# The opening of an edge-gated graph kernel, written in another order

## The chip, the core and the metric

The kernel runs on one core of one Trainium2 chip. Its time is the device time of one execution in microseconds (us); several executions are timed, and the median is given. A profile is one further execution, recorded by the hardware profiler. TensorE is PE in the profile (PEld is its weight load), VectorE is DVE, ScalarE is ACT, GpSimd is POOL, and SyncE, which only issues transfers here, is SP.

## The reference

There are 16 graphs (batch b) over the same 1024 nodes, with 256 features per node, and one adjacency matrix `adj` of 1024 x 1024 of which only some entries are not zero: about one in 128, and the diagonal.

```python
pre_u = einsum('bud,dk->buk', h, W1[:d]);  pre_v = einsum('bvd,dk->bvk', h, W1[d:])
hidden = relu(pre_u[:, :, None] + pre_v[:, None] + b1)
S = sigmoid(einsum('buvk,ko->buvo', hidden, W2)[..., 0] + b2)
a = einsum('buv,bud->bvd', S * adj, h)
m = einsum('uv,bud->bvd', adj, h) * h
z = beta1 * h + beta2 * (a @ Wa + ba) + beta3 * (m @ Wm + bm)
```

The gate S is only needed where `adj[u, v]` is not zero. So the kernel works on lists of edges.

## The kernel before, in words

The nodes v are cut into 8 tiles of 128 (`NT`), the 16 graphs into 4 groups of 4 (`GB`). A block is one group with one tile; there are 32. Each block takes ten steps (`T`), so the main loop (L745) has 320 steps. In a step, 128 edges, one in each partition, are worked on for four graphs at once: GpSimd gathers for each edge the row of its source node u from a table in DRAM (`fetch`, L494; a row holds `h W1[:d]` and `h` of the four graphs, 8 KB), TensorE spreads the rows of the target nodes v over the edges with a 0/1 matrix, the marks (`expand`, L564), DVE adds both and does relu and the product with W2 (`gate`, L598; L601 and L606), ACT does the sigmoid and scales the left factors (L609, L612), and TensorE sums the edges into their targets (`aggregate`, L614). Six fetches are under way at once (`NF`).

Before the first step, an opening of its own (L505 to L546) has to provide:

- **Edge lists** (`lists`, L239) of the first four tiles of v; the other four are made during the loop. A list is made in nine pieces, separated by `yield`: (1) the key is a row of 1024 adjacency entries per partition; DVE turns it into numbers (L249), ACT counts (L252); (2) DVE takes maxima in eight strips (L258); (3) DVE picks the top candidates and completes a tile `R` (L263 to L282); (4) TensorE sums over partitions (L286); (5) DVE computes the first slot and the number held (L291 to L309); (6) DVE writes the marks into a tile `made`, which has one buffer (L312, L319), ACT casts them to bytes (`few`, L329, two buffers), and DVE writes `RR` (L331); (7) four transfers write the bytes to `whose` (L335), TensorE multiplies the marks with `RR` (L338), ACT copies the product to `L` (L342); (8) DVE computes indices `uidx` and `vidx` (L346 to L364); (9) DVE writes one-hot rows (L370).
- **Row products** (`rows`, L434): for each of eight tiles of u, in two halves, TensorE multiplies `hT` with `w_u` (L427), and ACT copies the half out (L443). The finished tile is written to the table by SP (L446); the row of `h` itself gets there by a transfer from DRAM to DRAM (`copy_h`, L421).
- **Target rows of the first block** (`halves`, L452): two halves on TensorE with a bias product (L431, L427), each copied by ACT into `X` and `low` (L461, L462); then DVE subtracts (L463), and ACT writes the remaining three pieces of `X` (L465, L468).
- **Edge values** (`fetch_val`, L379): ten gathers by GpSimd of 128 adjacency values each.
- **Six fetches**, which wait until the whole table of the first group is in DRAM.

The order is written out by hand; nothing is rearranged later (`manual_schedule`, L471). Each engine works in order of issue, and a piece that waits holds what is behind it on its engine. The opening's order is the `script` (L518). A digit takes list 0 to 3 one piece further, `r` does one half of a row product, `h` one piece of `halves`, `v` the edge values (and the bias row `b1_p`, by `spread`, L190), and `f` issues the six fetches. What is registered with `after` for a step is done at that step's start; each string is one step. Row copies to the table are thus issued one step after a tile's second half. Of list 3 the last three pieces follow in loop steps 0, 2 and 4 (`advance`, L722).

The loads at the start are issued in the order of L508 to L513. The keys of lists 0 and 1 come by GpSimd's queue, those of lists 2 and 3 by SP's queue between the eight loads of `hT` (L241). After the script, `load_mark(0)` (L740) has ACT read the first marks back from `whose`, `expand` is called for steps 0 and 1, and the loop starts.

The PSUM banks `misc` (two) hold row products and halves, so the third product waits until ACT has copied the first. The banks `pc` (two) hold list products, and later the expansions.

Of the kernel before, what the change touches and what calls it, by code (L numbers as in the profile page):

```python
# [7 lines left out]
FP = mybir.dt.float32  # L8
FR = mybir.dt.float32r
# [4 lines left out]
P = 128  # L14
# [3 lines left out]
def kernel(  # L18
# [42 lines left out]
    nc = tc.nc  # L61
    B, N, D = x.shape
# [6 lines left out]
    NW = P // W  # L69
    TW = 5  # L70
    E = TW * P
# [113 lines left out]
    unit = fixed([P, P], "unit", FR)  # L185
# [9 lines left out]
    b1_p = fixed([P, D], "b1_p", FR)  # L195
# [6 lines left out]
    whose = const.tile([P, NT * NW, E], mybir.dt.uint8, name="whose")  # L202
# [9 lines left out]
    big = main.enter_context(tc.tile_pool(name="big", bufs=2))  # L212
# [4 lines left out]
    psa = main.enter_context(tc.tile_pool(name="psa", bufs=1, space=bass.MemoryType.PSUM))  # L217
# [12 lines left out]
    EARLY = 4  # L230
# [7 lines left out]

    def lists(vt):  # L239
        key = fetched[vt + 1][:, :N] if vt < EARLY else big.tile([P, N], FP, name="key", bufs=1)  # L240
        (nc.sync if 2 <= vt < EARLY else nc.gpsimd).dma_start(key, adjT[vt * P:(vt + 1) * P, :])  # L241
        yield "load"
        R = wk.tile([P, RC], FP, name="R", bufs=4)
        top = R[:, 5:5 + S]
# [2 lines left out]
        for c in range(0, N, N if vt < EARLY else N // 2):  # L247
            c = slice(c, c + (N if vt < EARLY else N // 2))
# [36 lines left out]
        for i in range(4):  # L285
            nc.tensor.matmul(pw[:, i:i + 1], sums[:, i].rearrange("p w q v -> p (w q v)"), R[:, 0:1],  # L286
                             start=True, stop=True)
# [23 lines left out]
        mark = big.tile([P, E], FP, name="made", bufs=1)  # L311
# [14 lines left out]
        RR = wk.tile([P, NW, RC], FP, name="RR", bufs=2)  # L326
        few = wk.tile([P, E], mybir.dt.uint8, name="few", bufs=2)
        yield "slot"
        nc.scalar.copy(few, mark)  # L329
        for w, mine in enumerate((soon, late)):  # L330
            nc.vector.tensor_scalar(RR[:, w, :], R, mine, None, ALU.mult)  # L331
        yield "step"
        for w in range(NW):
            for h in range(2):
                (nc.gpsimd if vt < EARLY else nc.scalar).dma_start(whose[h * W:(h + 1) * W, vt * NW + w, :], few[w * W:(w + 1) * W])  # L335
# [158 lines left out]
    def fetch(n):  # L494
        k, g, vt, w, j = where(n)
        nc.gpsimd.indirect_dma_start(  # L496
            out=fetched[n % NF], out_offset=None, in_=table[g],
            in_offset=bass.IndirectOffsetOnAxis(ap=uidx[:, vt * NW + w, j:j + 1], axis=0),
            bounds_check=N - 1, oob_is_err=False)
# [15 lines left out]
    for i in range(COPIES):  # L515
        copy_h(turn[i], nc.sync)

    script = ("r 0 0", "r r 0", "r 1", "0 r 1 1", "0 0 r r", "1 r 0 2 2", "r r 0 0 v 2", "1 1 r r",  # L518
              "2 r 1 r", "2 2 r r 1 1 h", "2 h 3 3", "2 2 h 3", "f h h 3", "3 3")
    m = 0  # L520
    piece = None
    parts = halves(0)
    for t, turns_ in enumerate(script):
        step = t - 100
        do(step)
        for c in turns_.split():
            if c == "r":
                if m % 2 == 0:
                    piece = rows(turn[m // 2], tabs[m // 2] if m // 2 < len(tabs) else None)
                    next(piece)  # L530
                go(piece, step)
                if m % 2 == 0 and m // 2 + COPIES < NT:
                    copy_h(turn[m // 2 + COPIES], nc.sync)
                m += 1
            elif c == "h":
                go(parts, step)
            elif c == "v":
                fetch_val(T)
                spread(b1_p, b1_b)
                next(parts)  # L540
            elif c == "f":
                for n in range(NF):
                    fetch(n)
            else:
                next(made[int(c)], None)
    do(len(script) - 100)  # L546
# [7 lines left out]

    marks, pcs, accs, evs, hbs, LTs, lefts = {}, {}, {}, {}, {}, {}, {}

    def load_mark(q):  # L560
        marks[q] = big.tile([P, E], FR, name="mark")
        nc.scalar.copy(marks[q], whose[:, order[q // NW][1] * NW + q % NW, :])  # L562

    def expand(n):  # L564
        k, g, vt, w, j = where(n)
# [171 lines left out]
    plan(again, ((103,), (113,), (125,), (133,)))  # L737
    begun = set(turn[:NT])
    end = parts = piece = last = None
    load_mark(0)  # L740
    for n in range(2):
        expand(n)
    left_adj(0)
# [200 lines left out]
```

## Time and profile before

| | |
|---|---|
| time, median of 3 runs | 1175.09 us (1167.8 to 1177.88) |
| span of the profiled execution, first to last instruction | 1165.8 us |
| PE, DVE, ACT, POOL busy | 1092.1, 1056.2, 893.5, 439.9 us |
| first `t` of the loop (L601) starts | 71.62 us |
| first, tenth after it, twentieth after it | 71.62, 112.31, 155.01 us |
| first fetch issued (L496) | 56.66 us |
| first product of TensorE (L427) | 5.94 us |

The page gives no time of its own for the profiled execution beside its span; the three timed runs lie 2.0 to 12.1 us above that span. A line of the timeline shows the start in us from the beginning of the span, the duration in us, engine, line, operation, output and input with sizes, how many instructions were merged, and in brackets how long the engine had been idle before, and what ended the wait. Where several conditions were waited for, the named one is the last by the profile. A windows line shows the stretch, its length, busy time of PE, PEld, DVE, ACT and POOL with the number of instructions, the granted TensorE clock as a share of full speed, the mean busy share of the 16 DMA engines, and GB/s.

### The profile page before, as it was taken

The numbers are of one execution on the slowest core, as the hardware profiler recorded it, in microseconds if no ns is written. First come the engines' busy times: TensorE is split into PE (matmuls) and PEld (weight loads), VectorE is DVE, ScalarE is ACT, GpSimd is POOL, SyncE is SP. The second block draws the span as 40 slices with busy tenths as digits, with TensorE's granted clock in tenths as the row PEclk, the third lists the DMA queues.
The fourth block names the chain that finished last, engine by engine and source line by source line (L and its number), as shares of the span: only waits on it lengthen the run. The fifth ranks groups of instructions, "written<-read, shape, count | busy, mean of one in ns | idle before, by whom it ended". The sixth has DMA issues, their size and how long they took to land. (4 is left out here: it accounts for less than half of the span.)

```text
span 1165.8 us, 23918 instructions
## 1 busy us (share of the span) xinstructions
PE 1092.1 (94%) x7633; PEld 723.1 (62%) x7633; DVE 1056.2 (91%) x3487; ACT 893.5 (77%) x2624; POOL 439.9 (38%) x428
## 2 busy tenths in 40 slices
PE   7867899999999999999999999999999999999986
PEld 6744666666666666666666666666666666666553
DVE  7688889888999989999999999999999999999994
ACT  2346587767887878888888888888888888888873
POOL 1556645253335333443333333333333333333330
PEclk9868899999999999999999999999999999999999
DMA  9986898999999999999999999999998998999991
GB/s 286 298 307 223 277 372 312 362 320 331 342 320 323 396 379 336 358 350 402 389 374 369 355 364 356 360 364 383 371 375 324 361 322 333 334 339 328 328 346 60
DMA packets 147048, 391.40 MB, mean 336 GB/s; under 512 B 16753, under 2 KB 105329, under 8 KB 110705
## 3 DMA queue, kind: packets, MB, share of 16 engines
q0 software_dynamic: 50016, 300.50, 68.9%
q1 hardware_dynamic: 81616, 74.99, 20.0%
q10 hardware_dynamic: 15280, 14.29, 3.7%
q8 instruction: 63, 1.03, 0.3%
q14 instruction: 73, 0.59, 0.1%
HBM read 393.78 MB, written 50.33 MB: 381 GB/s over the span
## 5 line engine op out<-in xcount | busy, mean ns | idle before, releaser
L496 POOL DMA_INDIRECT fetched<-table,uidx x320 | 341.5, 1067 | 628.3 <-PE acc L623 447.2
L606 DVE SCALAR_TENSOR_TENSOR t<-t,w_b 128x256 f32<-128x256 f32 x1280 | 478.3, 421 | 19.3 <-ACT left L612 0.5
L601 DVE TENSOR_TENSOR t<-fetched,pc 128x1024 f32<-128x1024 f32 x320 | 389.3, 1217 | 41.4 <-PE pc L569 13.9
L623 PE MATMUL acc<-fetched,left 128*32 128x256 f32 x4096 | 336.2, 391 | 31.9 <-ACT left L612 26.2
L612 ACT ACTIVATE left<-left,gt 128x32 f32<-128x32 f32 (+1 forms) x1280 | 299.3, 304 | 10.4
L569 PE MATMUL pc<-X,mark 128*128 128x512 f32 x640 | 237.6, 453 | 6.2 <-ACT mark L562 5.0
L623 PEld LDWEIGHTS acc<-fetched,left 128*32 128x32 f32 x4096 | 130.6, 109 | 179.3 <-issue 52.4
L569 PEld LDWEIGHTS pc<-X,mark 128*128 128x128 f32 x640 | 97.2, 191 | 140.0 <-issue 89.3
L609 ACT ACTIVATE gt<-sc,b_b 128x4 f32<-128x4 f32 x320 | 96.2, 301 | 43.4 <-DVE t L606 40.8
L672 PE MATMUL misc<-w_m,LT 128*128 128x256 f32 x496 | 117.2, 379 | 0.0
L672 PE MATMUL misc<-w_a,LT 128*128 128x256 f32 x496 | 117.1, 379 | 0.0
L579 ACT ACTIVATE left<-onehot,val 128x128 f32<-128x128 bf16 (+1 forms) x320 | 116.5, 364 | 0.0
L427 PE MATMUL misc<-w_v,hT 128*128 128x256 f32 x448 | 107.3, 383 | 0.0
L427 PE MATMUL misc<-w_u,hT 128*128 128x256 f32 x416 | 101.2, 390 | 5.7 <-ACT few L329 3.6
L606 DVE DVE_READ_ACCUMULATOR t<-t,w_b 128x1 f32 x1280 | 104.0, 81 | 0.0
L672 PEld LDWEIGHTS misc<-w_a,LT 128*128 128x128 f32 x496 | 93.9, 189 | 15.1
L672 PEld LDWEIGHTS misc<-w_m,LT 128*128 128x128 f32 x496 | 93.8, 189 | 14.9
L382 POOL DMA_INDIRECT val<-in_adjT_dram,vidx x80 | 85.7, 1071 | 35.1 <-issue 22.4
L427 PEld LDWEIGHTS misc<-w_v,hT 128*128 128x128 f32 x448 | 86.0, 192 | 13.9
L427 PEld LDWEIGHTS misc<-w_u,hT 128*128 128x128 f32 x416 | 79.5, 195 | 17.3 <-ACT few L329 3.7
L631 ACT COPY ev<-acc 128x512 f32<-128x512 f32 x128 | 75.5, 590 | 14.6 <-PE acc L623 4.2
L675 ACT COPY z<-misc 128x512 f32<-128x512 f32 x62 | 36.3, 586 | 58.1 <-PE misc L672 38.8
(164 smaller groups left out, 947.9 us busy)
## 6 DMA issues: line engine op xcount, KB each, us to landing
h_blk<-in_x_dram SPq DMA_DIRECT2D x31, 512.0 KB
out_dram<-z SPq DMA_DIRECT2D x31, 512.0 KB
hT<-in_xT_dram SPq DMA_DIRECT2D x28, 512.0 KB
table<-in_x_dram ACTq DMA_DIRECT2D x24, 512.0 KB
table<-tab SPq DMA_DIRECT2D x24, 512.0 KB
fetched<-table,uidx POOLq DMA_INDIRECT x320
table<-in_x_dram SPq DMA_DIRECT2D x8, 512.0 KB
table<-fetched SPq DMA_DIRECT2D x8, 512.0 KB
```

What stands on the lines that cost most here:

```text
L382: nc.gpsimd.indirect_dma_start(out=val[:, i, j:j + 1], out_offset=None, in_=adj_flat, in_offset=bass.IndirectOffsetOnAxis(ap=vidx[:, i, j: ...
L427: nc.tensor.matmul(p[:, bb * D:(bb + 1) * D], hT[:, 2 * h + bb, i, :], wt[:, i, :], start=(i == 0 and not begun), stop=(i == DC - 1), skip ...
L496: nc.gpsimd.indirect_dma_start(out=fetched[n % NF], out_offset=None, in_=table[g], in_offset=bass.IndirectOffsetOnAxis(ap=uidx[:, vt * NW ...
L569: nc.tensor.matmul(pcs[n][:, c], marks[n // TW][:, j * P:(j + 1) * P], cuts[k][:, w, c], start=True, stop=True)
L579: nc.scalar.activation(lefts[n][:, :m, :, 0, :], onehot[:, i, o:o + m, :].unsqueeze(2).to_broadcast([P, m, GB, V]), AF.Copy, scale=val[:, ...
L601: nc.vector.tensor_tensor(t, fetched[n % NF][:, :GD].rearrange("p (b d) -> p b d", b=GB), pcs.pop(n).rearrange("p (b d) -> p b d", b=GB), ...
L606: nc.vector.scalar_tensor_tensor(t[:, b, :], t[:, b, :], 0.0, w2_b, ALU.max, ALU.mult, accum_out=sc[:, b:b + 1])
L609: nc.scalar.activation(gt, sc, AF.Sigmoid, bias=b2_b)
L612: nc.scalar.activation(lefts[n][:, :m, b, 1, :], lefts[n][:, :m, b, 0, :], AF.Copy, scale=gt[:, b:b + 1])
L623: nc.tensor.matmul(accs[h][b * 2 * V:(b + 1) * 2 * V, r, :], left[:, i, b].rearrange("p k v -> p (k v)"), f[:, GD + b * D:GD + (b + 1) * D ...
L631: nc.scalar.copy(evs[q], accs.pop(q))
L672: nc.tensor.matmul(pz[:, bb * D:(bb + 1) * D], LTs[k][:, c, 2 * h + bb, i, :], wt[:, c, :], start=False, stop=(i == 0 and c == DC - 1), sk ...
```

## The change

The change concerns the opening alone.

- The key of list 0 is loaded by SP, ahead of the `hT` loads, and no longer by GpSimd.
- For the first four lists the cast of the marks to bytes is done by GpSimd, in piece 7 ahead of the four transfers, and no longer by ACT in piece 6. The later four lists are unchanged.
- The script has another order. Halves of row products stand ahead of list products, `f` comes before list 2's seventh piece, and there are 16 steps instead of 14.
- `load_mark(0)` is called from the script (`m`), between the pieces of `halves` and the fourth piece of list 3.
- A new letter, `w`, issues six TensorE products of `unit` with the bias row into a bank of the accumulator `acc0`; nothing reads them. It comes four times, all after list 2's L338: three times before list 3's L286, and once between that and the first expansion.

```diff
     def lists(vt):
         key = fetched[vt + 1][:, :N] if vt < EARLY else big.tile([P, N], FP, name="key", bufs=1)
-        (nc.sync if 2 <= vt < EARLY else nc.gpsimd).dma_start(key, adjT[vt * P:(vt + 1) * P, :])
+        (nc.sync if vt in (0, 2, 3) else nc.gpsimd).dma_start(key, adjT[vt * P:(vt + 1) * P, :])
...
         yield "slot"
-        nc.scalar.copy(few, mark)
+        if vt >= EARLY:
+            nc.scalar.copy(few, mark)
         for w, mine in enumerate((soon, late)):
             nc.vector.tensor_scalar(RR[:, w, :], R, mine, None, ALU.mult)
         yield "step"
+        if vt < EARLY:
+            nc.gpsimd.tensor_copy(few, mark)
...
-    script = ("r 0 0", "r r 0", "r 1", "0 r 1 1", "0 0 r r", "1 r 0 2 2", "r r 0 0 v 2", "1 1 r r",
-              "2 r 1 r", "2 2 r r 1 1 h", "2 h 3 3", "2 2 h 3", "f h h 3", "3 3")
+    script = ("0 r 0 r", "1 r 0", "r 1 r 0", "r 0 0", "1 r r", "0 r 2", "1 r 0 0", "r 1 2 r", "1 2 r v", "3 r 1",
+              "2 r 1 1", "r 2 2", "h 3 f", "h 2 w", "2 2 3 h h h w", "m w 3 3 3 w")
...
+    def warm(times):
+        spare = psa.tile([P, 2, D], FP, name="acc0")
+        for i in range(times):
+            nc.tensor.matmul(spare, unit, b1_p.unsqueeze(1).to_broadcast([P, 2, D]), start=True, stop=True)
...
+            elif c == "m":
+                load_mark(0)
+            elif c == "w":
+                warm(6)
...
-    load_mark(0)
     for n in range(2):
         expand(n)
```

`load_mark` itself is unchanged; its definition is moved ahead of the script. In the changed kernel the lines of the loop are 11 or 12 higher: `gate` adds at L613, and the fetch is L499.

More of the change, by code (lines that the diff above doesn't have):

```diff
@@ L516, with load_mark @@
         copy_h(turn[i], nc.sync)
-    script = ("r 0 0", "r r 0", "r 1", "0 r 1 1", "0 0 r r", "1 r 0 2 2", "r r 0 0 v 2", "1 1 r r",
-              "2 r 1 r", "2 2 r r 1 1 h", "2 h 3 3", "2 2 h 3", "f h h 3", "3 3")
+    script = ("0 r 0 r", "1 r 0", "r 1 r 0", "r 0 0", "1 r r", "0 r 2", "1 r 0 0", "r 1 2 r", "1 2 r v", "3 r 1",
+              "2 r 1 1", "r 2 2", "h 3 f", "h 2 w", "2 2 3 h h h w", "m w 3 3 3 w")
+    marks, pcs, accs, evs, hbs, LTs, lefts = {}, {}, {}, {}, {}, {}, {}
+    def load_mark(q):
+        marks[q] = big.tile([P, E], FR, name="mark")
+        nc.scalar.copy(marks[q], whose[:, order[q // NW][1] * NW + q % NW, :])
+    def warm(times):
+        spare = psa.tile([P, 2, D], FP, name="acc0")
+        for i in range(times):
+            nc.tensor.matmul(spare, unit, b1_p.unsqueeze(1).to_broadcast([P, 2, D]), start=True, stop=True)
     m = 0
@@ L553, in scale_late @@
         nc.vector.tensor_scalar(w_m, w_m, be3, None, ALU.mult)
[L558 to L562, printed above, removed]
     def expand(n):
```

## The prediction

> **What bounds the kernel now.** The page's chain that ended last covers 1% of the span, so I read the stage that the change touches. The page's busy shares (PE 94%, DVE 91%) are those of the 320-step loop, which the change leaves as it is; what can move is the moment at which the loop starts. In the timeline that is the first `t` of `gate` on DVE (L601), at 71.62 us, and the last one is followed by the same work in both kernels. So I listed the DVE timeline up to there and kept the rows with idle time in front. Columns: start, duration, operation, and in brackets the idle time before it and what ended it.
>
> ```profile
> 9.69 1.22 DVE L249 SCALAR_TENSOR_TENSOR fetched<-fetched,ukey 128x1024 f32<-128x1024 f32 x1 [2.29 <-DMA fetched<-in_adjT_dram]
> 29.91 0.17 DVE L346 TENSOR_TENSOR s_of<-slot_of,L 128x10 f32<-128x10 f32 x1 [3.04 <-ACT L L342]
> 47.50 0.55 DVE L312 TENSOR_SCALAR made<-upto,R 128x640 f32<-128x640 f32 x1 [5.51 <-PE pc L338]
> 57.51 1.23 DVE L463 TENSOR_TENSOR low<-low,X 128x1024 f32<-128x1024 f32 x1 [2.33 <-ACT low L462]
> 65.44 0.28 DVE L291 TENSOR_SCALAR from<-misc,base,low__108 128x1 f32<-128x1 f32 x1 [1.89 <-PE misc L286]
> 71.62 1.22 DVE L601 TENSOR_TENSOR t<-fetched,pc 128x1024 f32<-128x1024 f32 x1 [2.04 <-PE pc L569]
> ```
>
> The six waits sum to 17.1 us. Without any of them DVE would reach the first gate at 71.6 - 17.1 = 54.5 us: no order of this opening can gain more than 17 us. Next I asked who made DVE wait, on the other engines:
>
> ```profile
> 40.81 3.78 PE L427 MATMUL misc<-w_u,hT 128*128 128x256 f32 x8 [3.62 <-ACT few L329]
> 70.36 2.07 PE L569 MATMUL pc<-X,mark 128*128 128x512 f32 x4 [4.96 <-ACT mark L562]
> 39.55 0.72 ACT L329 CAST few<-made 128x640 uint8<-128x640 f32 x1 [5.97 <-issue]
> 68.95 0.72 ACT L329 CAST few<-made 128x640 uint8<-128x640 f32 x1 [7.24 <-DVE made L319]
> 56.66 1.07 POOL L496 DMA_INDIRECT fetched<-table,uidx  x1 [4.42 <-DMA table<-fetched]
> ```
>
> ACT stands at a cast of list marks (L329); the copies that empty TensorE's banks queue behind it, TensorE stands 3.62 us, and DVE waits 5.51 us for list products (L338) behind those row products. At the end the first `load_mark` (L562) waits behind the last cast, and TensorE's first expansion starts at 70.36. Last the windows of the opening (busy us per engine, then granted clock, DMA share, GB/s):
>
> ```profile
> 20.00:40.00 20.00, 16.06 (x79) 14.02 (x78) 15.77 (x71) 5.35 (x10) 7.45 (x10) 0.88 1.08 322
> 40.00:60.00 20.00, 15.55 (x70) 13.38 (x70) 11.50 (x44) 9.63 (x18) 11.72 (x16) 0.84 0.85 268
> 60.00:72.00 12.00, 3.48 (x12) 2.94 (x12) 7.41 (x38) 4.59 (x6) 5.92 (x8) 0.50 0.92 368
> ```
>
> TensorE is nearly idle from 60 on and its clock is at 0.50. The DMA engines are full until about 47.
>
> **What the Trainium skill says.** "TensorE: Matmul & The Clock Gate", Part 1: the array runs at half clock after an idle window of about 3.4 us and at full clock after as much work. The trace agrees: 16 products of L427 took 6.32 us at 5.94 and 3.69 us at 13.02. "DMA: Bandwidth & Descriptors", Queues, rings and completion order: each DMA engine takes turns between the queues that have work. The trace fits: `hT__180`, first on SP, was used at 5.94 while GpSimd's first transfer, also 512 KB, was used at 9.69. "GPSIMD Engine Reference", 3.1: a one-input body runs between 1.03 and about 1.8 cycles per element at 1.2 GHz. For 640 elements I estimate 0.55 to 1.0 us; no GpSimd cast is in the trace. "SBUF — State Buffer", two separate sides: GpSimd and two-input DVE operations exclude each other for a whole instruction; no row here shows it.
>
> **The change, part by part.** I walk TensorE and DVE in the new order of issue with these durations: half a row product 1.81 (24 products in 5.43), the first two 6.32; L286 1.05; L338 1.35; a half of `halves` 2.37 (L431 0.48 and four L427 products, 1.89); on DVE L249 1.25, maxima 1.65, top candidates to `R` 2.19, first/held 1.88, marks and RR 2.16, indices and one-hots 2.68, `spread` 1.04, `low` 1.23.
>
> *Key of list 0 on SP ahead of hT.* It lands by DVE's end of set-up at 7.4, so the 2.29 wait goes. But hT__180 is now second on SP. By 10 us SP had moved 0.93 MB before, and it now needs 1.05 MB; GpSimd has one key less to compete with. I take 10.0 for TensorE's start (5.94 before; bounds 7.5, if the 4 KB rows of the key pass quickly, and 11). The key of list 1 is first on GpSimd, where it lands as list 0's did, at 9.7: no wait.
>
> *Row products first.* TensorE: 10.0 + 6.32 + 3.69 + 1.81 + 1.05 = 22.9, when list 0's L286 is done. DVE had been ready at 15.4 (7.4, then L249, maxima, L249, candidates, maxima): a new wait of 7.5 us, the largest left. Then DVE 1.88 + 2.16 to 27.0; TensorE 28.3 after three halves, L338 to 29.7, and so on without a stall: 32.5 at list 1's L286, 41.6 with row 6 done, 42.9 L338, 44.0 list 2's L286, 47.6 the last row product. Before, ACT copied that one out at 51.4 to 52.0.
>
> *ACT.* The cast is gone, but the count of list 3 (L252) stands ahead of the copy of row 6's second half and waits for DVE's L249 at 43.3. List 1's L is copied at 45.5, DVE waits 2.3 us for it, and runs 48.3, 50.2, 52.3, 54.0 (list 3's maxima).
>
> *X and the idle products.* `halves` ends on TensorE at 52.3, list 2's L338 at 53.7. Three groups of six products follow: 18 x 0.365 (two L569 took 0.73) = 6.6 us, to 60.3. DVE does `low` at 54.0 to 55.2, indices to 57.9, list 3's candidates to 60.1. So the idle products cost 0.2 us on the path; their cover is DVE's 2.68 + 2.19. If each took 0.48 as one L431 did, they would cost 2.3. List 3's L286 ends at 61.3, DVE 1.88 + 2.16 to 65.4: first gate at **65.5**. The fourth group and the first expansion, 2.2 + 0.75 after 61.3, end at 64.3, hidden by 1.2.
>
> *First marks early.* `load_mark` needs list 0's marks only, and follows the low parts of X (55.2 + 2.1) at about 58: hidden.
>
> *Casts on GpSimd.* 0.9 each (0.55 to 1.4 with dispatch). List 0's and 1's stand by the ten val gathers (1.3 each) and are done by 48, two us before DVE rewrites `made`. List 2's stands behind the six fetches. The last table write leaves ACT at 48.2 and lands 4.7 later as before (52.0 to 56.66): 52.9. By 50 us 15.05 MB had been moved, of 15.4 MB that precede the fetches, so it can't land much before 52. Six fetches take 8.15 (56.66 to 64.81), the cast ends at 62.0, and DVE's L312 of list 3 needs it at 63.3: hidden by 1.3 us. Behind it on GpSimd are the DMAs of marks, the next key and the loop's gathers; DVE waits for the cast, nobody for those at once. List 3's cast adds 0.9 to GpSimd's queue in the first step.
>
> *The loop's start.* The clock is now warm where it was 0.52 (70 to 80). The gates of steps 0 to 5 are paced by DVE, busy 9.63 of 10 us from 80 to 90, so I count nothing for it, against the 0.9 of list 3's cast.
>
> Sum: 71.6 - 65.5 = **6.1 us** off the span of 1165.8. The runs are 2.0 to 12.1 above the span, with the median at 1175.1, so the prediction is 1175.1 - 6.1 = 1169.0 us.
>
> **The rivals.** (a) *More gain:* hT__180 lands at 7.5, all of TensorE's walk comes 2.5 earlier, and the warm clock also saves step 6's wait of 1.80 for a cold expansion (1.22 instead of 0.73) and the GpSimd fetch's 3.06 at 81.23. 6.1 + 2.5 + about 3.5 = 12: 1163. For it: SP's queue starts with long rows. Against: the full DMA engines.
> (b) *The gain is given back* in the first 30 steps, where GpSimd issues two gathers and a fetch per step at 1.3 each, 3.9 us against 3.43 in the mean of the loop, and the fetches must land. The gates there come every 4.1 us (71.62 to 112.31, ten steps). If GpSimd's queue, and not its start, sets this: 1174. Against: GpSimd too starts its fetches 3.8 earlier.
> (c) *Slower:* list 2's cast behind the fetches holds DVE. If the last table write lands at F, the first gate is at F + 8.15 + 0.9 + 2.16. It decides from F = 54.3, and the kernel is slower than before from F = 60.4. At F = 64, 11 us later than worked out, it gives 1179. Against: the DMA engines have no more bytes than before.
> (d) *The idle products don't warm but delay:* at the 0.77 that a cold L431 took at 75.90, 18 take 13.9 and the gate comes at 72.8: 1176. Against: TensorE works without pause up to them.
>
> **How the numbers follow.** Forecast 0.48, (a) 0.19, (b) 0.17, (c) 0.11, (d) 0.05. About 1% (11.8 us) is what a measurement of this kernel tells from no change, since its three runs spread by 10 us. Faster than 1163.3 are half of (a) and the edge of the forecast when run spread helps: 0.16. Slower than 1186.8 takes a bad (c): 0.07. The range 1160 to 1178 holds all but the tails of (a) and (c); its ends are the 12 us of (a) less 3 of run spread, and (d) or a mild (c).
>
> **What would show it.** In the profile after: the first L613 at 63 to 68; TensorE's first product at 8 to 11; a DVE wait of 5 to 8 us for list 0's L286 near 23; no wait of ACT for marks; a clock near 1.0 from 50 to 66; the first fetch at 52 to 54; casts on POOL below 1.4. Wrong it would be if casts are several us long, if DVE waits for POOL at L312, or if the gates of steps 10 and 20 lie no earlier than 112.31 and 155.01.

## The result, and the profile after

The changed kernel takes 1174.96 us in the median of 22 runs (1167.54 to 1179.61), the kernel before 1171.96 us in 22 runs on the same chip (1166.21 to 1177.88). The ratio is 1.0026, with a 95% interval of 1.0009 to 1.0043: a loss of 3 us, small, but the interval does not reach 1. Forecast was a gain of 6.1 us. The profiled execution of the changed kernel took 1175.41 us with a span of 1173.0.

The DVE timeline up to the first gate, rows with idle time in front, and the first gate itself (L613):

```profile
24.01 0.28 DVE L291 TENSOR_SCALAR from<-pc,base,low__108 128x1 f32<-128x1 f32 x1 [8.95 <-PE pc L286]
49.57 0.17 DVE L349 TENSOR_TENSOR s_of<-slot_of,L 128x10 f32<-128x10 f32 x1 [4.98 <-ACT L L345]
66.55 0.28 DVE L291 TENSOR_SCALAR from<-misc,base,low__108 128x1 f32<-128x1 f32 x1 [2.60 <-PE misc L286]
71.11 1.21 DVE L613 TENSOR_TENSOR t<-fetched,pc 128x1024 f32<-128x1024 f32 x1
```

Six waits with 17.1 us in sum have become three with 16.5. The first gate moved by 0.5 us, from 71.62 to 71.11, where 65.5 was forecast. TensorE, in its own timeline:

```profile
12.86 5.15 PE L430 MATMUL misc<-w_u,hT__180 128*128 128x256 f32 x16 [12.86 <-DMA hT__180<-in_xT_dram]
...
58.33 7.39 PE L532 MATMUL acc<-b_p,unit 128*128 128x512 f32 x18
65.56 0.95 PE L286 MATMUL misc<-R,sums 128*128 128x1 f32 x8
...
67.84 1.09 PE L581 MATMUL pc<-X,mark 128*128 128x512 f32 x4
```

The first product came at 12.86, not at 10.0. The expansions (L581) were done 2.2 us ahead of the first gate: the wait for a late, cold expansion is gone. The windows of the opening (busy us of PE, PEld, DVE, ACT, POOL; granted clock, DMA share, GB/s) show the same:

```profile
20.00:40.00 20.00, 20.00 (x107) 17.95 (x106) 14.94 (x67) 7.08 (x13) 7.21 (x10) 1.00 1.06 331
40.00:60.00 20.00, 15.09 (x74) 12.66 (x73) 14.07 (x57) 7.22 (x13) 13.25 (x14) 0.92 0.92 273
60.00:72.00 12.00, 8.82 (x33) 6.06 (x32) 8.66 (x39) 4.41 (x6) 7.17 (x10) 0.85 1.00 400
```

TensorE is full and warm from 20 to 40 and at 0.85 instead of 0.50 from 60 to 72. The opening looks better, and the kernel is slower. The place to look is GpSimd, after the six fetches. Its timeline:

```profile
55.47 1.23 POOL L499 DMA_INDIRECT fetched<-table,uidx  x1 [4.25 <-DMA hT__767<-in_xT_dram]
...
63.91 0.73 POOL L335 CAST few<-made 128x640 uint8<-128x640 f32 x1
64.94 2.29 POOL L338 DMA_DIRECT2D whose<-few  x4 [0.30 <-POOL few L335]
70.17 0.72 POOL L335 CAST few<-made 128x640 uint8<-128x640 f32 x1 [2.94 <-DVE made L319]
71.18 0.52 POOL L338 DMA_DIRECT2D whose<-few  x1 [0.29 <-POOL few L335]
72.79 0.52 POOL L338 DMA_DIRECT2D whose<-few  x1 [1.09 <-DMA fetched<-table,uidx]
75.53 0.52 POOL L338 DMA_DIRECT2D whose<-few  x1 [2.22 <-DMA fetched<-table,uidx]
79.41 0.52 POOL L338 DMA_DIRECT2D whose<-few  x1 [3.37 <-DMA fetched<-table,uidx]
79.92 0.57 POOL L241 DMA_DIRECT2D key<-in_adjT_dram  x1
80.79 1.08 POOL L385 DMA_INDIRECT val<-in_adjT_dram,vidx  x1 [0.30 <-issue]
82.17 1.02 POOL L385 DMA_INDIRECT val<-in_adjT_dram,vidx  x1 [0.30 <-issue]
83.49 1.00 POOL L499 DMA_INDIRECT fetched<-table,uidx  x1 [0.30 <-issue]
```

The same stretch in the kernel before, whose first fetch is at 56.66:

```profile
69.97 2.14 POOL L335 DMA_DIRECT2D whose<-few  x4 [5.16 <-ACT few L329]
72.16 0.57 POOL L241 DMA_DIRECT2D key<-in_adjT_dram  x1
74.57 1.07 POOL L382 DMA_INDIRECT val<-in_adjT_dram,vidx  x1 [1.84 <-DMA fetched<-table,uidx]
77.16 1.02 POOL L382 DMA_INDIRECT val<-in_adjT_dram,vidx  x1 [1.52 <-DMA fetched<-table,uidx]
81.23 0.99 POOL L496 DMA_INDIRECT fetched<-table,uidx  x1 [3.06 <-PE pc L569]
```

There list 3's four transfers are issued together, and the fetch of step 6, the first that the loop itself issues, leaves at 81.23. Here three of the same four wait for fetches to land, 1.09, 2.22 and 3.37 us, and the fetch of step 6 comes at 83.49. Counting what GpSimd issues from the first fetch on makes the difference plain. In both kernels the first eleven leave without such a wait, the 12th, 13th and 14th stand, and the 14th leaves at 81.23 before and at 79.41 after. But the 14th is the fetch of step 6 in the kernel before, while in the changed kernel list 2's four transfers have been put in front, so it is the 18th, four places or 4.1 us after the 14th. From there to 95.7 GpSimd does not pause: two value gathers and a fetch per loop step, 1.3 us each. Later it does, for up to 2 us at a time.

| gate of step | 0 | 4 | 5 | 10 | 12 | 20 | 31 |
|---|---|---|---|---|---|---|---|
| before | 71.62 | 84.93 | 90.21 | 112.31 | 120.76 | 155.01 | 196.38 |
| after | 71.11 | 84.41 | 92.42 | 114.02 | 122.35 | 157.89 | 203.01 |

The changed kernel is 0.5 us ahead until step 4 and behind from step 5, by 1.6 to 2.9 us up to step 20 in the table. The step at which it falls behind, and what more is lost between steps 20 and 31, belong to this pair of executions: in the second pair of profiles, below, it is ahead until step 7 (94.29 against 96.93) and behind from step 8 (104.67 against 103.36), and the distance at step 31 is 2.9 us (203.12 against 200.24).

### The profile page after: what moved, and what is told of

It is laid out like the page before. It is cut to its first block, busy times and chain, and to the rows that moved or that the text cites. A ratio compares the mean times of both kernels' runs of the same rounds, so it can differ in the third digit from the quotient of the medians.

```text
span 1173.0 us, 23972 instructions
## 1 busy us (share of the span) xinstructions
PE 1095.9 (93%) x7657; PEld 725.2 (62%) x7657; DVE 1056.1 (90%) x3487; ACT 890.8 (76%) x2620; POOL 443.6 (38%) x431
## 5 line engine op out<-in xcount | busy, mean ns | idle before, releaser
L499 POOL DMA_INDIRECT fetched<-table,uidx x320 | 342.5, 1070 | 630.7 <-PE acc L635 455.7
L613 DVE TENSOR_TENSOR t<-fetched,pc 128x1024 f32<-128x1024 f32 x320 | 389.3, 1217 | 46.2 <-PE pc L581 14.3
L581 PE MATMUL pc<-X,mark 128*128 128x512 f32 x640 | 235.1, 449 | 6.8 <-DVE t L613 3.8
L581 PEld LDWEIGHTS pc<-X,mark 128*128 128x128 f32 x640 | 96.2, 189 | 139.8 <-issue 93.1
L656 ACT COPY LT<-misc 128x512 f32<-128x512 f32 x128 | 70.5, 575 | 19.2 <-remote 6.2
```

Source lines behind the costliest of these rows:

```text
L499: nc.gpsimd.indirect_dma_start(out=fetched[n % NF], out_offset=None, in_=table[g], in_offset=bass.IndirectOffsetOnAxis(ap=uidx[:, vt * NW ...
L581: nc.tensor.matmul(pcs[n][:, c], marks[n // TW][:, j * P:(j + 1) * P], cuts[k][:, w, c], start=True, stop=True)
L613: nc.vector.tensor_tensor(t, fetched[n % NF][:, :GD].rearrange("p (b d) -> p b d", b=GB), pcs.pop(n).rearrange("p (b d) -> p b d", b=GB), ...
```

## Experiments

Theory Q: the loss comes from GpSimd's order. List 2's transfers stand behind the fetches, list 3's wait for landings, so the queue of value gathers and fetches starts late; its length sets the gates until about step 20. The rivals are named in each expectation. Every ratio is against the kernel before, run on the same chip in the same comparison. One thing has to be known to read the tables: in the second comparison the kernel before took 1148.69 us, in the others 1169 to 1173, on that same chip too; so times are compared within a comparison only. What makes these two levels is not known.

**First comparison: one edit each on the changed kernel** (kernel before 1171.89 us).

*Fetches behind list 2's transfers.*

```diff
-"h 3 f", "h 2 w"
+"h 3", "h 2 f w"
```

> The changed kernel with the six fetches (L499) issued behind the cast and the four transfers of list 2's bytes on GpSimd, the order that the kernel before had. Theory Q (GpSimd's queue): in the changed kernel these four transfers stand behind the fetches, so list 3's transfers, the next key and the first value gather wait for fetches to land, and the fetch of step 6 comes at 83.5 instead of 81.2; that loses what the gates lose from step 5 on (7 us between the profiles, 3 between the medians). Then here list 2's cast is done by 57.3, its transfers by 59.6, the first fetch at 59.8, the first value gather at 75 to 77, the gates of steps 10 and 20 lie 1.5 to 3 us earlier against the first gate than in the changed kernel, and the median is 2 to 4 us below it, at or under the kernel before. Rival S (spread from execution to execution, the loop's own): the first gate stays at 71.1, later gates move by as much as any two executions differ, and the time is that of the changed kernel, ratio 1.002 to 1.003. Rival F (the fetches matter more): fetches 4.3 us later hold the first gates, first gate at 73 or later, ratio 1.004.

Measured: 1171.18 us, 0.9995 (0.9974 to 1.0016). GpSimd:

```profile
57.23 2.05 POOL L338 DMA_DIRECT2D whose<-few  x4 [0.29 <-POOL few L335]
59.71 1.18 POOL L499 DMA_INDIRECT fetched<-table,uidx  x1 [0.44 <-DMA be<-in_beta_dram]
...
70.44 2.14 POOL L338 DMA_DIRECT2D whose<-few  x4 [0.30 <-POOL few L335]
72.56 0.57 POOL L241 DMA_DIRECT2D key<-in_adjT_dram  x1
75.05 1.10 POOL L385 DMA_INDIRECT val<-in_adjT_dram,vidx  x1 [1.91 <-DMA fetched<-table,uidx]
77.52 1.04 POOL L385 DMA_INDIRECT val<-in_adjT_dram,vidx  x1 [1.38 <-DMA fetched<-table,uidx]
81.22 0.99 POOL L499 DMA_INDIRECT fetched<-table,uidx  x1 [2.66 <-DVE vidx L367]
```

List 3's transfers are again issued in one piece, and the fetch of step 6 is the 14th entry again and back at 81.22, though the first fetch starts 4.2 us later than in the changed kernel. The first gate did not suffer (70.37), so rival F falls. Steps 10 and 12 came 2.2 and 2.1 us earlier than in the changed kernel. Step 20 did not (160.64): that execution took 1177.55 us, 6 above its median, and ACT stood 6.55 us at 130.44 with no engine named. So the fetch of step 6 alone does not fix step 20. The median speaks for Q: the 3 us are back, though the interval still overlaps a little with that of the changed kernel (1.0009 to 1.0043).

*Lists 2's and 3's transfers on SP.*

```diff
-(nc.gpsimd if vt < EARLY else nc.scalar).dma_start(whose[...], ...)
+(nc.gpsimd if vt < 2 else nc.sync if vt < EARLY else nc.scalar).dma_start(whose[...], ...)
```

> The changed kernel with the eight transfers of list 2's and 3's bytes issued by SP instead of GpSimd; the casts stay on GpSimd, list 2's behind the fetches. Theory Q: GpSimd has nothing that waits for a fetch's landing before the key; the key is issued at 71.5, the first value gather at 73 to 76, the fetch of step 6 at 79 to 81, with the fetches still starting at 55.5; gates 10 and 20 lie 2 to 4 us earlier than in the changed kernel (114.02 and 157.89), the median 3 to 5 us below it. Rival S: the first gate is at 71.1, and the time is that of the changed kernel. Rival R (SP): the transfers stop SP, which waits for list 3's cast until 70.9 with the loop's first load of hT behind it; that load is used only from step 5 on, so at most 1 us is lost.

Measured: 1167.93 us, 0.9967 (0.9950 to 0.9984); first value gather at 70.69, fetch of step 6 at 79.33, gates 10 and 20 at 110.47 and 154.78. Q's direction and more than its size: 7 us below the changed kernel. The fetch of step 6 is now the tenth entry and waits for no landing, but 6.29 us for the sums of step 0, whose buffer it takes. It is no clean proof, because SP now waits for the casts, and its loads behind them (`hT`, `w_a`, `w_m`, some 1.5 MB) start at 72.39 instead of 50.95, behind list 3's cast (69.16), so they no longer move at the same time as the fetches. The two effects were not separated.

*No idle products.*

```diff
-                warm(6)
+                pass
```

> The changed kernel without the 24 idle products (L532). Theory I (they are on the path): list 3's L286 starts when DVE has finished R, near 63.9 instead of 65.56, DVE's wait for it falls from 2.60 to about 1.0, and the first gate is at 69.0 to 69.6. They give nothing back, because TensorE's clock is low from 72 to 76 in either kernel: the median is 1 to 2 us below the changed kernel. Rival W (they warm): without them list 3's L286, the first expansions and the sums of steps 0 to 4 run at half clock, the first gate stays at 71 or the gates of steps 1 to 5 come 1 to 2 us later, and the time is the same as the changed kernel's or above it.

Measured: 1173.42 us, 1.0023 (1.0006 to 1.0040), first gate 70.89. This is rival W's outcome: L286 of list 3 starts earlier, at 64.45 instead of 65.56, but takes 1.84 us instead of 0.95. What the idle products hold back they give back.

*Key of list 0 back on GpSimd.*

```diff
-nc.sync if vt in (0, 2, 3) else nc.gpsimd
+nc.sync if vt in (2, 3) else nc.gpsimd
```

> The changed kernel with the key of list 0 back on GpSimd, so that hT__180 is first on SP again. Theory K (the key in front of hT cost TensorE's start): TensorE's first product at 6 to 7 instead of 12.86, DVE's L249 of list 0 with a wait of 2 to 3 us, list 0's L286 done at 18 to 19 instead of 24.0, DVE's wait for it 2 to 4 instead of 8.95. What follows is then limited by the loads of hT (rows 6 and 7) and by ACT: the last table write and the first fetch come 1 to 3 us earlier (52.5 to 54.5), the first gate at 67 to 69. The loop gives part of it back on GpSimd's queue: median 0 to 3 us below the changed kernel. Rival D (the DMA engines set the opening): the loads of the later hT land no earlier, the row products of tiles 6 and 7 run when they ran, the first gate is at 70.5 to 71.5, and the time is unchanged.

Measured: 1172.39 us, 1.0014 (0.9995 to 1.0032). TensorE's timeline:

```profile
5.81 6.21 PE L430 MATMUL misc<-w_u,hT__180 128*128 128x256 f32 x16 [5.81 <-DMA hT__180<-in_xT_dram]
```

TensorE starts 7 us earlier, and the first gate comes at 65.28, 5.8 us earlier than in the changed kernel; rival D falls. The key's new place had cost most of this: of the 5.8 us, DVE's waits for list 0 make 4.8 (2.69 for the key and 1.44 for L286 here, against 8.95), the rest lies behind them. But the time hardly moves: the fetch of step 6 comes at 81.70, behind the same waits for landings, and step 12's gate at 122.11, as in the changed kernel. A first gate that is 6 us earlier is worth 1.4 us by the ratios here, which the intervals do not tell from nothing.

**Second comparison** (kernel before 1148.69 us).

*Key of list 0 on GpSimd, and transfers on SP: both edits above.*

> The changed kernel with the key of list 0 back on GpSimd and the transfers of list 2's and 3's bytes on SP, the two edits together. Each alone showed a half: with the key moved back the first gate came at 65.28, but GpSimd's queue was still behind (fetch of step 6 at 81.70) and step 12's gate was at 122.1, as in the changed kernel; with the transfers on SP the first gate stayed at 70.10, the fetch of step 6 came at 79.33, and step 12's gate at 118.8. Theory Q (from step 5 to step 30 GpSimd's queue of two value gathers and a fetch per step, 3.9 to 4.0 us, sets the gates, so an earlier first gate counts only if GpSimd's first value gather and the fetch of step 6 move with it): first gate at 64 to 66, fetch of step 6 at 73 to 76, step 12's gate at 113 to 116, median 1162 to 1165. Rival P (the fetches' landing or TensorE sets steps 5 to 12): step 12's gate at 118 to 120, median 1167 to 1169, no better than with the transfers on SP alone.

Measured: 1144.96 us, 0.9964 (0.9945 to 0.9982); first gate 64.70, fetch of step 6 at 74.55, step 12 at 113.70. The early events came as Q said, the time did not: the ratio is that of the transfers on SP alone, in time rival P's outcome. The profile names two new waits. DVE stands 2.79 us for list 2's cast, which is behind the fetches, at 62.09: the wait of my rival (c). Then the gate of step 4 waits 4.51 us, until 82.51, because an ACT-issued transfer of the loop (L424) leaves only at 77.28 and the sigmoids stand behind it.

*The kernel before with those transfers on SP.*

> The kernel before with the transfers of list 2's and 3's bytes on SP, all else as it was. Theory Q: there list 2's transfers stood ahead of the fetches, and list 3's waited for no fetch (2.14 us at 69.97), so SP saves GpSimd 2 to 3 us around 70, of which it waits part for fetches in any case; the fetch of step 6, which waited 3.06 us for TensorE at 81.23, moves by 0 to 2 us, and the median is 0 to 2 us below the kernel before. Rival X (GpSimd's transfers cost the same in any order): the gain is as large as in the changed kernel, 6 to 7 us.

Measured: 1148.72 us, 0.9995 (0.9971 to 1.0018), fetch of step 6 at 80.98. There, where list 2's four transfers had stood ahead of the fetches, the same edit gains nothing; rival X falls. The fetch of step 6 waits 13.65 us there for the sums of step 0, so it is the first steps of the loop that hold it, and not GpSimd's queue.

*The changed kernel again.*

> The changed kernel once more, for a second profile of it. Theory Q: what is due to the order repeats, so the first gate is at 70.5 to 71.5, the first value gather after the fetches at 79 to 82, the fetch of step 6 at 82 to 85, step 12's gate at 122 to 123.5; what differs between executions beyond step 28 (a wait of 2.9 us near 190 in the first profile) need not repeat. Rival S (spread): step 12's gate lies anywhere between 119 and 124. The median is 1173 to 1175 in either case.

Measured: 1151.69 us, 1.0029 (1.0011 to 1.0048): the loss is there on this chip too. First gate 67.46, 3 us earlier than expected: DVE's three waits are 9.24, 2.05 and 1.07 us here, where the first profile had 8.95, 4.98 and 2.60. The first value gather is at 79.29 and the fetch of step 6 at 82.20, so GpSimd's start hardly moved with the first gate.

*The kernel before with the casts on GpSimd alone.*

```diff
-        nc.scalar.copy(few, mark)
+        if vt >= EARLY:
+            nc.scalar.copy(few, mark)
...
+        if vt < EARLY:
+            nc.gpsimd.tensor_copy(few, mark)
```

> The kernel before with the first four lists' casts on GpSimd, all else as it was. Theory C (the casts on ACT made the wait of 5.51 us for list products and the late first marks): DVE's wait near 47.5 falls to 2 to 4 us, list 3's cast no longer stands in front of the first marks on ACT, the first gate moves from 71.62 to 67 to 70. By theory Q GpSimd then sets the steps after: list 2's transfers are ahead of the fetches, list 3's cast adds 0.7 us to GpSimd in front of the next key, so step 12's gate stays within 1.5 us of 120.76 and the median within 2 us of the kernel before. Rival E (the opening's end counts in full): the median is 2 to 4 us below the kernel before.

Measured: 1147.14 us, 0.9993 (0.9975 to 1.0011); first gate 64.66, fetch of step 6 at 77.93, step 12 at 110.81. DVE's wait near 44 is now 4.62 us, for a GpSimd cast behind value gathers instead of for list products. Against the other kernel of this comparison that has the old script (transfers on SP, first gate 72.18) the casts alone bring the first gate 7.5 us forward, more than the whole change does; in the pair with one gather, below, it is 3.5 (71.41 and 67.94). Steps 12 and 20 are 5.3 and 3.3 us earlier. Of this the median shows 1.6 us, within the intervals. That step 12 would stay was wrong.

In this comparison GpSimd had no pause of its own between the fetches of steps 6 and 21, 15 steps, in three of the four kernels (58.8, 58.0 and 58.0 us), and step 20's gate came 65.9, 65.9 and 65.7 us after the fetch of step 6 (82.20, 80.98, 77.93). This is Q's carrying-over in its plainest form. In the profiles of the first and fourth comparisons with two gathers the same distance is 73.4 to 79.4 us, and GpSimd pauses in between; there something else holds the gates too.

**Third comparison: half the value gathers** (kernel before 1172.93 us). No gather is left out: the 70 that the loop makes are spread over more steps, and each still stands ahead of its use.

```diff
-            fetch_val(2)
+            fetch_val(1)
```

*In the changed kernel:*

> The changed kernel with one value gather per loop step instead of two; each gather still stands ahead of the step that uses it. Theory Q (GpSimd's queue of two value gathers and a fetch, 3.9 us a step, carries the time of the fetch of step 6 over to step 20): GpSimd's share falls to 2.6 us a step, it waits again between steps 6 and 20, the gates from 6 to 20 are paced by DVE and TensorE (about 3.4 us a step, 48 us for 14 steps, instead of 53 to 61), and the median falls by 4 to 9 us: ratio to the kernel before 0.995 to 0.999, where the changed kernel has 1.003. Rival T (TensorE and its clock set the early steps, GpSimd merely keeps up): gates 6 to 20 take 53 us or more, ratio 1.002 to 1.004.

*In the kernel before:*

> The kernel before with one value gather per loop step instead of two. Theory Q: gates 6 to 20 take about 48 us, ratio 0.992 to 0.997. With the queue no longer full, the changed order's loss of 2.3 us in the fetch of step 6 is caught up in part, so the distance between this kernel and the changed kernel with one gather is smaller than 3 us. Rival T: ratio 0.998 to 1.002, distance 3 us as before.

*In the changed kernel with the key of list 0 on GpSimd and the fetches behind list 2's transfers:*

> The changed kernel with the key of list 0 on GpSimd, the fetches behind list 2's transfers, and one value gather per step. The first part moved the first gate by 6 us without any gain in time while GpSimd's queue was full. Theory Q: now an earlier first gate counts; the first gate is 4 to 6 us earlier than in the changed kernel with one gather on the same chip, step 20's gate 3 to 6 us earlier, ratio 0.988 to 0.993. Rival A (the loop takes up any earlier start: the fetches' landing, ACT or TensorE hold steps 0 to 20 in another way): step 20's gate within 1.5 us of that of the changed kernel with one gather, ratio 0.995 to 0.999.

*In the kernel before with the casts on GpSimd:*

> The kernel before with the first four lists' casts on GpSimd and one value gather per step, the other parts of the change left out. The casts alone moved the first gate to 64.66 on a chip where the changed kernel's came at 67.46, with a time within 0.1% of the kernel before. Theory Q: first gate near 64 to 67, step 20's gate 3 to 6 us ahead of the kernel before with one gather, ratio 0.988 to 0.993, at or below every kernel so far. Rival A: ratio that of the kernel before with one gather, within 0.2%.

| one gather per step in | first gate | gate of step 20 | median us | ratio (interval) |
|---|---|---|---|---|
| the kernel before | 71.41 | 144.60 | 1151.06 | 0.9818 (0.9788 to 0.9848) |
| the changed kernel | 70.38 | 143.79 | 1148.71 | 0.9800 (0.9768 to 0.9831) |
| before, casts on GpSimd | 67.94 | 141.27 | 1147.34 | 0.9777 (0.9743 to 0.9812) |
| changed, key and fetches moved | 65.79 | 138.03 | 1144.40 | 0.9757 (0.9727 to 0.9787) |

The gain is 22 us and more, far above the 4 to 9 expected. Gates 6 to 20 take 52 us in the changed kernel (91.75 to 143.79) instead of 61; 48 was expected. With the queue short, the four kernels stand in the order of their first gates, and 5.6 us of first gate are worth 6.7 us of time; single intervals overlap, the order of all four is the argument. The changed order is now ahead of the kernel before, by 2.4 us. The windows from 90 to 150, the changed kernel first, then the same with one gather:

```profile
90.00:110.00 20.00, 13.27 (x74) 7.36 (x73) 12.74 (x48) 10.54 (x30) 13.70 (x14) 0.89 0.76 243
110.00:130.00 20.00, 14.79 (x91) 9.11 (x90) 15.89 (x54) 10.34 (x33) 14.66 (x14) 0.88 0.79 272
130.00:150.00 20.00, 18.10 (x106) 12.92 (x106) 16.88 (x62) 12.30 (x35) 11.68 (x11) 0.87 0.67 207
```

```profile
90.00:110.00 20.00, 17.35 (x112) 11.31 (x113) 19.47 (x79) 15.44 (x47) 13.44 (x14) 0.91 0.88 308
110.00:130.00 20.00, 18.29 (x112) 12.60 (x111) 19.34 (x65) 12.12 (x37) 10.88 (x11) 0.83 0.93 337
130.00:150.00 20.00, 20.00 (x143) 13.56 (x142) 16.75 (x58) 16.38 (x47) 11.93 (x13) 1.00 0.99 344
```

DVE works 55.6 of the 60 us instead of 45.5, TensorE 55.6 instead of 46.2.

These gains are those of the slower level, where the kernel before takes 1169 to 1173 us. The changed kernel with two gathers in the second comparison has these windows:

```profile
90.00:110.00 20.00, 15.21 (x102) 9.33 (x101) 16.29 (x68) 14.63 (x41) 15.43 (x15) 0.91 0.87 297
110.00:130.00 20.00, 17.58 (x114) 12.25 (x112) 18.97 (x65) 12.46 (x38) 15.67 (x15) 0.91 0.91 289
130.00:150.00 20.00, 19.70 (x141) 13.23 (x140) 15.64 (x50) 16.11 (x45) 13.51 (x15) 1.00 0.89 315
```

DVE works 50.9 us of 60 there, with GpSimd's queue full. The last step's gate comes at 1125.35 in this profile and at 1125.80 in that of the kernel before with the casts on GpSimd; with one gather, on the same chip, it comes at 1123.56 and 1125.85. So at the faster level one gather per step promises 0 to 2 us and not 22. That is read across two comparisons; beside each other the two were not run at that level.

**Fourth comparison** (kernel before 1170.34 us): the kernel before and the changed kernel once more, and the last kernel with two gathers and with one.

> The kernel before once more, for a profile of it beside the other three of this comparison. Theory Q (the time of the fetch of step 6 on GpSimd is carried over to step 20): fetch of step 6 at 80 to 82, step 20's gate 66 to 74 us after it. Ratio 1.000.

> The changed kernel once more, beside the kernel before with a profile of both. Theory Q: first gate 0 to 4 us ahead of that of the kernel before, fetch of step 6 still 1 to 3 us behind, at 82 to 84, step 20's gate 1 to 4 us behind. Ratio 1.002 to 1.004. Rival S (spread): the order of the two at step 20 is not that of the fetch of step 6.

> The changed kernel with the key of list 0 on GpSimd and the fetches behind list 2's transfers, with two value gathers per step as in the changed kernel. Theory Q: first gate 4 to 6 us ahead of the changed kernel's, but GpSimd's queue full, so what counts is the fetch of step 6: it waits for the fetches' landing and comes at 77 to 79, 3 to 5 us ahead of the changed kernel's; step 20's gate is ahead by the same, and the ratio is 0.996 to 0.999. Rival G (the first gate counts in full): ratio 0.994 or less. Rival N (nothing of it counts, as with the key alone): 1.001 to 1.003.

> The same with one value gather per step, repeated beside its own kernel with two gathers. Theory Q with a full queue in steps 6 to 20 (and what else waits while it is full): the gap between the two is 10 to 25 us where the kernel before takes about 1172 us, ratio 0.975 to 0.985. Rival L (the earlier gap of 28 us was a different level of the chip at that time, not the gathers): the gap is 5 us or less, ratio 0.992 or more.

| | first gate | fetch of step 6 | step 12 | step 20 | median us | ratio (interval) |
|---|---|---|---|---|---|---|
| kernel before | 71.83 | 81.09 | 121.48 | 154.50 | 1171.34 | 1.0006 (0.9985 to 1.0026) |
| changed kernel | 69.15 | 82.51 | 121.19 | 158.08 | 1174.62 | 1.0026 (1.0008 to 1.0044) |
| key and fetches moved | 65.54 | 77.51 | 117.39 | 153.19 | 1168.62 | 0.9989 (0.9968 to 1.0010) |
| the same, one gather | 65.97 | 73.87 | 110.19 | 139.55 | 1144.94 | 0.9778 (0.9742 to 0.9814) |

Step 20's gate repeats within 0.5 us in both kernels (155.01 and 154.50; 157.89 and 158.08), so rival S falls, and its order is that of the fetch of step 6, against the order of the first gates. The third row bears out Q's early events and its range, apart from the first gate (3.6 us ahead instead of 4 to 6); how much of the 5 us of GpSimd's start reach the end the intervals don't tell. The last row is 23.7 us below its own kernel with two gathers: rival L falls. 13.6 us of this are there at step 20, 21.4 in the last step's gate (1143.22 against 1121.81). Of the first part the queue's length explains some: at the faster level, with the queue full, gates 0 to 20 take 80.7 us in the changed kernel, against 73.4 with one gather, which is 7 us. The rest goes with waits of ACT. The kernels of this comparison with two gathers have such waits of 3 to 8 us between 90 and 140 for which the profile names no engine (7.65 us ahead of 131.56 in the changed kernel), and the one with a single gather has none over 2.6 us there. In the second comparison none of the four kernels with two gathers has one, and in three of them the queue was as full. So a full queue alone does not cause these waits; what does is open, and with it most of the 22 us.

**Two terms of the opening**, in the fastest kernel (kernel before 1168.90 us). First, list 3's first piece behind list 1's indices:

```diff
-"3 r 1", "2 r 1 1", "r 2 2"
+"r 1", "2 r 1 1", "3 r 2 2"
```

> The fastest kernel so far (key of list 0 on GpSimd, fetches behind list 2's transfers, one value gather per step; first gate 65.79 and 65.97, ratio 0.9757 and 0.9778), with list 3's first piece moved behind list 1's indices. Theory O (ACT's order: the count of list 3, L252, stands in front of the copy of list 1's product and of row products, and DVE waits 4 to 5 us for that product): DVE's wait near 44 falls to 1 to 2 us, the first gate comes 2 to 4 us earlier, at 62 to 64, and the ratio is 0.973 to 0.975. Rival N (ACT's copies are late there for a reason that is not the count, since the profile names no releaser for part of the delay): the wait stays at 3 to 5 us or comes back at the next product, first gate at 65 to 66.5, ratio unchanged.

Measured: 1144.28 us, 0.9771 (0.9735 to 0.9806), first gate 66.85, DVE's wait 3.54 us at 45.29. Theory O falls. ACT ahead of the copy of list 1's product (44.85), in this kernel:

```profile
42.16 0.59 ACT L446 COPY fetched<-misc 128x512 f32<-128x512 f32 x1 [7.50 <-remote]
```

With the count (L252) out of the way, ACT still stands 7.50 us in front of a copy of a row product, and the profile names no engine. The kernel before had such a wait too, 5.97 us ahead of its cast at 39.55, marked "issue". Its cause is left open.

Second, the fastest kernel without idle products (the edit shown above):

> The fastest kernel so far without the 24 idle products. Theory I (they hold list 3's L286; DVE waited 2.40 us for it at 61.41): the first gate comes 0.5 to 1.5 us earlier, and since GpSimd's queue no longer sets steps 6 to 20, this counts: ratio 0.975 to 0.977. Rival W (what they hold back they give back, because L286 takes 1.84 us at the low clock instead of 0.95): first gate within 0.5 us, ratio unchanged at 0.976 to 0.978.

Measured: 1142.81 us, 0.9762 (0.9727 to 0.9797), first gate 65.80. Rival W: no difference.

## Why the prediction was wrong

It missed by 9.1 us: -6.1 forecast, +3.0 measured. By the first pair of profiles the first gate accounts for 5.6 (71.11 against 65.5), the loop's start for the other 3.5. Item 4 below is the step that turned a smaller gain into a loss; items 1 to 3 are sizes that were off.

1. *"I take 10.0 for TensorE's start (5.94 before; bounds 7.5 ... and 11)".* The step that failed first. It was 12.86, and 11.73 to 12.85 in the other kernels of the first comparison with this placement, outside the bounds. DVE's wait for list 0's L286 was 8.95 us instead of 7.5, and 8.71 to 9.85 in all the profiles with this placement. The working saw that this part of the change buys a 2.3 us wait with a longer one, yet did not ask what the opening would be without it. The run with the key back on GpSimd says it: 65.28, that is 5.8 us of first gate, of which DVE's waits for list 0 make 4.8. That this kernel meets the 65.5 of the forecast is chance: TensorE starts there at 5.81, not at 10.0.
2. *ACT: "DVE waits 2.3 us for it".* 4.98 us in the first profile, and 4.77 to 5.05 in the others of the changed kernel and its variants with this placement, but for the second comparison, where it was 2.05, as worked out. I read ACT's stop before the cast at 39.55 as the cast's doing, and put what is left down to the count in front. But the wait was marked "issue", that is, nothing in the profile explained it; it reappears without cast and without count. A wait without a releaser can't be removed on paper.
3. *Idle products, "6.6 us ... cost 0.2 us on the path".* They took 7.39, and DVE's wait for list 3's L286 was 2.60 instead of 1.2 (61.3 - 60.1). With the two above, these waits add up to 5.5 of the 5.6. But the 2.60 is this one profile's: in the other two of the changed kernel the wait is 1.07 and 1.11, as worked out, with first gates at 67.46 and 69.15. And taking the products away changed nothing: their cost is that of a cold L286 (1.84 against 0.95) in another place. The rest was right: casts of 0.72 us, no wait for marks, expansions hidden, no wait of DVE for list 2's cast. One term was put at nothing without a reason: the exclusion of GpSimd and DVE, which the prediction names. It shows just ahead of the first gate: DVE's L324 of list 3, two operands of 128x1, starts at 70.30, inside GpSimd's cast (70.17 to 70.89), and takes 0.60 us until the cast's end, against 0.16 in the kernel before.
4. *"Behind it on GpSimd are the DMAs of marks, the next key and the loop's gathers; DVE waits for the cast, nobody for those at once", and "I count nothing" for the loop's start.* The step that turned the sign. I counted instructions on GpSimd, 0.9 us for a cast, and not what each transfer behind the fetches has to wait for. The kernel before showed it at 74.57 and 77.16 already: value gathers waiting 1.84 and 1.52 us for fetches. Moving four transfers behind the fetches moves list 3's into these waits, and the fetch of step 6 from the 14th place to the 18th, from 81.23 to 83.49 (82.20 and 82.51 in the other two profiles, with first gates 3.7 and 2.0 us earlier).
5. Rival (b), with 0.17, came nearest, with 1174: GpSimd's queue sets the early gates. But it has the gain given back only; that the queue's part of the loop starts later, which makes a loss of it, it does not say. My argument against it, that GpSimd "too starts its fetches 3.8 earlier", was wrong twice. The fetches started 1.2 us earlier, and not they but the work behind them decides. The row "3.9 us against 3.43 in the mean of the loop" was the sign to follow: in the stretch after the opening GpSimd's queue was at its limit, and little of a gain of the first gate could be counted there.
6. Rivals (a), (c) and (d) did not come about; (c)'s wait was seen once (2.79 us), when TensorE started early and the fetches still stood in front of the cast.

## What to carry to other kernels

When an opening is reordered, follow the engine that is the bound of the stretch after it, and date the step of that engine from which the loop runs, here the fetch of step 6, rather than the first step of the loop. Of a queue that issues transfers, count the entries as well as their time: behind the six fetches it was the place in the queue that decided which entries waited for a landing, and four small transfers put in front of the step that mattered pushed it back by four places. Then ask which work in that stretch has no hurry: one gather per step instead of two, still in time for its use, took 1.8% off the kernel before (0.9818), and with list 0's key where it was and the fetches behind list 2's transfers the changed order made 2.2 to 2.4% of it (0.9778 and 0.9757). Before such a gain is put down to the queue, look whether the waits that vanish are the queue's: here a good part was not, and where the kernel before takes 1149 us little of the gain is to be expected.

## What was not expected of the hardware

- A transfer of 40 KB that GpSimd issues in 0.52 us waited up to 3.37 us for the landing of an earlier fetch. Counted from the first of the six fetches, of the first twenty entries in GpSimd's queue only the tenth to the fourteenth ever waited for the landing of a fetch, in all 20 profiles, whatever these entries were.
- One 512 KB key in front of `hT__180` on SP's queue delayed it by 7 us (12.86 against 5.81), while with the key on GpSimd's queue beside it DVE waited only 2.7 us for that key.
- A cast of 128x640 on GpSimd (0.72 us) held a DVE operation that fell into it until its end: L324, 128x1, took 0.60 us instead of 0.16.
- The same idle products took 7.39, 6.53, 6.46 and 5.10 us for 18 (the changed kernel, transfers on SP, fetches late, key on GpSimd), and taking them away moved the time in neither of the two kernels in which it was tried.
- One value gather of 128 entries per step instead of two, 1.3 us of GpSimd, was worth 21.9 us in the kernel before and 23.7 in that with key and fetches moved, at the slower level. With it go waits of ACT for which no engine is named; at the faster level these are missing with two gathers as well.
